# Head of a two-block transformer kernel: row copies on ScalarE, a norm product on GpSimd, ordered first loads, and unread TensorE products

## The chip, the cores and the metric

The kernel runs on one core of a Trainium2 chip. A core has five engines, each with its own queue of instructions: TensorE (PE, matrix products; its weight loads are listed apart as PEld), VectorE (DVE), ScalarE (ACT), GpSimd (POOL) and SyncE (SP), which here only issues DMA transfers. An engine works through its own queue in order, and instructions on different engines wait for each other through semaphores. TensorE reads its operands from SBUF and writes to PSUM, which has eight banks.

The metric is the device time in microseconds (us) of one run; the median over several runs is compared. One execution is recorded by the hardware profiler, and every duration quoted comes from it. The profile also shows the TensorE clock that was granted at each moment, as a share of full speed: 1.0 is full, 0.5 is half.

## The reference

The input is `x` of shape 32 x 64 x 512 (32 sequences of 64 tokens), one position for each token, and a conditioning vector of 512 numbers for each sequence. Everything is fp32. Two blocks follow each other:

```
# block 0
n(x, w, tw) = x * rsqrt(mean(x*x) + 1e-6) * (w * (1 + cond @ tw.T))
h = n(x, ln1_w, ln1_tw)
q, k, v = h @ Wq.T (8 heads of 64), h @ Wk.T, h @ Wv.T (one head)
q, k = rope(q, positions), rope(k, positions)
x = x + softmax(q k' / 8) v @ Wo.T
h = n(x, ln2_w, ln2_tw)
x = x + (silu(h @ Wg.T) * (h @ Wu.T)) @ Wd.T        # 512 -> 2048 -> 512
# block 1
scale, shift = split(cond @ W_ada.T + b_ada)
h = layernorm(x) * (1 + scale) + shift
q, c = h @ Wq.T (16 heads of 32), h @ Wkd.T (128)
k, v = c @ Wku.T, c @ Wvu.T (4 heads each)
x = x + softmax(rope(q) rope(k)' / sqrt(32)) v @ Wo.T
```

The four vectors that depend on `cond` (the scale of each of the two norms of block 0, and scale and shift of block 1) are called modulations 0 to 3 in the kernel.

## The kernel before, in words

**Tiling.** The 2048 tokens are cut into eight units of 256 tokens (four sequences). Channels lie on the 128 partitions, so a unit of `x` is a tile of 128 x 4 chunks x 256 tokens. Products are made in pieces: 128 x 128 weights against 256 tokens in the attention, against 128 in the MLP. The gate, up and down products of the MLP are computed by a scheme of seven products on blocks in place of eight. It needs sums and differences of weight blocks; `combine` (L255 to L258) makes them when a "set" of weights is used for the first time, in the first unit, and keeps them in DRAM. The sets pass through a ring of five buffers, tag `mw`. The first four weight tiles of the modulations (0 and 1) and the first sets share that ring.

**Stages.** The *head* is what runs before the first MLP product: modulations 0 to 3, the rotation angles, and block 0's attention for units 0 and 1. Then `Order().run` works through the MLP of unit after unit, with the attention of the neighbouring units woven in by estimated costs. The *tail* is block 1's attention for the last two units.

**What orders the head.** Three generators hand out TensorE work in pieces: `a` (attention of unit 0), `b` (attention of unit 1) and `m` (modulations 1 to 3). The string `FIRST` (L49) says in which order the next piece of each is taken, and the block `with ordered(tc, PE)` (L1045 to L1047) pins TensorE to that order. Modulation 0 stands before it. On the other four engines a scheduler orders the instructions, those of SP, which issues the transfers, among them.

**The parts that the text below speaks of**, with their lines in the kernel before:

- L152 to L154: eleven products of the constant tile `ones` with itself at the start; nobody reads the result.
- L175 (positions), L180 (`small`: conditioning vectors, mask and other small constants, 138 KB), L276 (weights of a modulation, two halves of 512 KB), L215 (`x` of a unit, 512 KB), L284 (`wqkv`: the weights of queries, keys and values, two tiles), L287 (`wo0`, 1 MB): the first loads. L242, L245 and L247 load the sets of MLP weights (L245 the block called `a21`).
- L290 to L315, `modulation`: sixteen products into `ps_mod` (L296), a copy of the result to SBUF as `rows` (L304), a transpose on TensorE (L307) and one VectorE instruction that leaves the modulation in its fixed tile (L311, L313 or L315).
- L364 to L395, `first_angles`: the angles of units 0 and 1, twenty small instructions on VectorE and ScalarE; L392 to L394 are `Abs` and the two sines, L395 the sine's sign.
- L498 to L520, `rms`: the square of `x` on ScalarE (L500) and the product of `x` and the modulation (L508). In the head ("lean") that product is made in two halves, one on VectorE and one on GpSimd, and the row factor, one over the root, is applied later (L521).
- L478, `root_by_quarters`: means over channels (`ms_a0` for unit 0) as small products; L470 the square root, L471 the reciprocal.
- L413 to L429, `tables_by_quarters`: L416 multiplies angles by the row factor, then TensorE spreads them (`tab`, `row`), and ScalarE copies them (L425, L426, L428).
- L525, `project`: the products of `kv`, `q` and `po` (the output projection). L533 to L536 rotate; L536, on GpSimd, leaves `qT`. L545 to L555 are the softmax. L673 are the scores. L560 are the transposes of the softmax result, `pp`. L573 adds `po` to `x`.
- L899 and L958: gate and up (`gu`) and down products of the MLP. L845, L869 and `lat` belong to block 1's attention.

**PSUM banks.** `abank(name)` hands out a bank from a list of homes in turn. In the head and in the tail the list is ("at", "gu", "acc", "acc"), in between it is "at" alone. How many tiles the head has taken therefore decides which home a later tile gets.

Of the kernel before, what the change touches and what calls it, by code (L numbers as in the profile page):

```python
# [17 lines left out]
P = 128  # L18
B, S, D = 32, 64, 512
T = B * S  # L20
KC = D // P
# [24 lines left out]
ROUND = 12582912.0  # L46
WARM = 11
STAY = 14103
FIRST = "aaaaaaa bb a mm aa bb a bbb aa b mm a bb aa a m b a b m b a b".replace(" ", "")  # L49
TWO_PI = float(np.nextafter(np.float32(2 * np.pi), np.float32(0)))  # L50


# [43 lines left out]
@contextmanager  # L96
def ordered(tc, engine):

    traced = tc.nc.cur_bb.bb.instructions
    start = len(traced)  # L100
    yield
    mine = [i for i in traced[start:] if i.engine == engine]
    info = mybir.DependencyInfo(mybir.DependencyClass.NoSync, mybir.DependencyReason.DATA)
    for one, other in zip(mine, mine[1:]):
        tc.add_manual_dep(other, one.name, info, reason="order")
# [3 lines left out]
def two_blocks(ctx: ExitStack, tc: tile.TileContext, a: dict, out: bass.AP):  # L109
    nc = tc.nc  # L110
# [8 lines left out]
    def bank(tag, name):  # L119
        return psum.tile([P, 512], F32, tag=tag, name=name, bufs=BANKS[tag])  # L120
# [12 lines left out]
    def fixed(shape):  # L133
        n, i = int(np.prod(shape[1:])), stays["at"]
        stays["at"] += n
        assert stays["at"] <= STAY
        t = stays["all"][:, i : i + n]
        if len(shape) == 2:
            return t
        names = "abc"[: len(shape) - 1]  # L140
        return t.rearrange(f"p ({' '.join(names)}) -> p {' '.join(names)}", **dict(zip(names, shape[1:])))

    def work(tag, shape, name, bufs=2):
        return wk.tile(shape, F32, tag=tag, name=name, bufs=bufs)
# [3 lines left out]
    make_identity(nc, ident)  # L148
    ones = fixed([P, P])
    nc.gpsimd.memset(ones, 1.0 / D)  # L150

    idle = bank("at", "idle")  # L152
    for _ in range(WARM):
        nc.tensor.matmul(idle[:, :P], ones, ones, start=True, stop=True)  # L154

    spread = fixed([P, US, P])
    nc.gpsimd.memset(spread, 0.0)
    for q in range(US):
        rows = slice(q * HALF0, (q + 1) * HALF0)
# [13 lines left out]
    def load_positions(u0):  # L173
        t = work("pos", [P, 2 * S], f"pos_{u0}", 1).bitcast(I32)
        nc.sync.dma_start(t, a["pos"][:, u0 * S : (u0 + 2) * S])  # L175
        positions.append(t)

    load_positions(0)
    small = fixed([P, C_ALL])
    nc.sync.dma_start(small, a["small"])  # L180
# [87 lines left out]
    def load_mod(i):  # L268

        mods.append({})  # L270
        for j, tag in enumerate((("mw", "mw"), ("mw", "mw"), ("h2", "h2"), ("sq", "td"))[i]):
            bufs = {"sq": 1, "mw": MW}.get(tag, 2)
            some = KC // 2 if tag == "td" else KC
            for k0 in range(0, KC, some):
                t = work(tag, [P, some, D // 2], f"mod_{i}_{j}_{k0}", bufs)
                nc.sync.dma_start(t, a["mod"][i][:, k0 : k0 + some, j * 256 : (j + 1) * 256])  # L276
                for k in range(some):
                    for c in range(2):
                        mods[i][2 * j + c, k0 + k] = t[:, k, c * P : (c + 1) * P]
# [5 lines left out]
    load_x(1)  # L285
    load_mod(1)
    nc.sync.dma_start(wo0, a["wo0"])  # L287


    def modulation(i):  # L290

        dst = (s0a, s0b, s1, t1)[i]
        ps = abank(f"ps_mod{i}")
        for k in range(KC):
            for c in range(KC):
                nc.tensor.matmul(  # L296
                    ps[c * B : (c + 1) * B, :P],
                    condT[:, k, :],
                    mods[i][c, k],
                    start=(k == 0),  # L300
                    stop=(k == KC - 1),
                )
        rows = work("latT1", [P, UT], f"rows_{i}", 1)[:, :P]
        nc.vector.tensor_copy(rows, ps[:, :P])  # L304
        yield 1.2, 0.5
        pt = abank(f"pt_mod{i}")
        nc.tensor.transpose(pt[:, :P], rows, ident)  # L307
        got = pt[:, :P].rearrange("p (c b) -> p c b", b=B)
        v = vecs[:, KC * i : KC * (i + 1)].unsqueeze(2).to_broadcast([P, KC, B])
        if i < 2:  # L310
            nc.vector.scalar_tensor_tensor(dst, got, 1.0, v, ALU.add, ALU.mult)  # L311
        elif i == 2:
            nc.vector.scalar_tensor_tensor(dst, got, 1.0, v, ALU.add, ALU.add)  # L313
        else:
            nc.vector.tensor_tensor(dst, got, v, ALU.add)  # L315
        yield 0.1, 0.0
# [115 lines left out]
    def per_seq(s, u):  # L432

        return s[:, :, US * u : US * (u + 1)].unsqueeze(3).to_broadcast([P, KC, US, S])

    def by_seq(ap):
        return ap.rearrange("p c (b s) -> p c b s", s=S)
# [14 lines left out]
    def tile4(room, tag, name):  # L452
        return space(room, tag, KC * UT, name).rearrange("p (c t) -> p c t", t=UT)

    def total_of(room, t, name):

        total = space(room, "tot", UT, f"tot_{name}")
        nc.gpsimd.tensor_tensor(t[:, 0:2], t[:, 0:2], t[:, 2:4], ALU.add)
        nc.gpsimd.tensor_tensor(total, t[:, 0], t[:, 1], ALU.add)
        return total  # L460

    def mean_of(parts, name):

        ps = abank(name)
        for k, part in enumerate(parts):
            nc.tensor.matmul(ps[:, :UT], ones, part, start=(k == 0), stop=(k == len(parts) - 1))
        return ps[:, :UT]

    def inverse_root(mean, eps, r):
        nc.scalar.activation(r, mean, AF.Sqrt, bias=eps)  # L470
        nc.vector.reciprocal(r, r)  # L471

    def root_by_quarters(parts, eps, r, name):

        ps = abank(name)
        for k, part in enumerate(parts):
            for b in range(US):
                nc.tensor.matmul(  # L478
                    ps[b * HALF0 : (b + 1) * HALF0, :S],
                    ones[:, :HALF0],  # L480
                    part[:, b * S : (b + 1) * S],
                    start=(k == 0),
                    stop=(k == len(parts) - 1),
                )
        inverse_root(ps[:, :S], eps, r)
# [9 lines left out]
    def rms(u, s, h, room, name):  # L495

        x = x_units[u]
        lean = "lean" in room  # L498
        sq = tile4(room, "h", f"sq_{name}") if lean else work("sq", [P, KC, UT], f"sq_{name}", 1)
        nc.scalar.activation(sq, x, AF.Square)  # L500
        if lean:
            parts = [sq[:, k] for k in range(KC)]
            c = KC // 2
            for e, part in ((nc.vector, slice(0, c)), (nc.gpsimd, slice(c, KC))):
                to = h[:, part].rearrange("p c (b s) -> p c b s", s=S)
                of = x[:, part].rearrange("p c (b s) -> p c b s", s=S)
                by = s[:, part, US * u : US * (u + 1)].unsqueeze(3).to_broadcast([P, c, US, S])
                e.tensor_tensor(to, of, by, ALU.mult)  # L508
            yield 0.0, 1.5
        else:  # L510
            parts = [total_of(room, sq, name)]
            nc.gpsimd.tensor_tensor(by_seq(h), by_seq(x), per_seq(s, u), ALU.mult)
            yield 0.0, 6.0
        if lean:
            return parts
        r = space(room, "r", UT, f"r_{name}")
        inverse_root(mean_of(parts, f"ms_{name}"), eps0, r)
        return r
# [61 lines left out]
    def attention0(u, room, early=None, late=None):  # L580
# [17 lines left out]
        def keys_values():  # L598
            kv = abank(f"kv0_{u}")
            project(kv[:, :UT], wqkv[0], slice(2 * P, 3 * P), h)  # L600
            return kv
# [7 lines left out]
        if lean:  # L609
            few = space(room, "few", 3 * S, f"quarters_{u}").rearrange("p (k c) -> p k c", c=S)  # L610
            root_by_quarters(r, eps0, few[:, 0], f"ms_a{u}")
            kv = keys_values()
            yield 1.7, 0.0
            turn = query(0)
            yield 3.4, 0.0
# [43 lines left out]
        if lean:  # L659
            ps = [space(room, "p", 512, f"p0_{u}_{t}") for t in range(2)]  # L660
        else:
            both = space(room, "p", 1024, f"p0_{u}")
            ps = [both[:, t * 512 : (t + 1) * 512] for t in range(2)]

        for ts in ((0,), (1,)) if lean else ((0, 1),):
            banks = [abank(f"sc0_{u}_{ts[0]}_{r}")[:, : 256 * len(ts)] for r in range(2)]
            for n in range(KC * len(ts)):
                t, c = ts[n // KC], n % KC
                for b in range(2):
                    cols = slice((2 * t + b) * S, (2 * t + b + 1) * S)  # L670
                    for r, sc in enumerate(banks):
# [5 lines left out]
                            start=True,  # L677
                            stop=True,
# [352 lines left out]
    for _ in modulation(0):  # L1031
        pass
# [7 lines left out]
    streams = {  # L1040
        "a": attention0(0, {"ring": "0", "lean": True, "p": [first[:, :512], first[:, 512:]]}, early),
        "b": ahead.pieces,
        "m": other_mods(),
    }
    with ordered(tc, mybir.EngineType.PE):  # L1045
        for name in FIRST:
            next(streams[name], None)  # L1047
    rest = [ahead]
    for w, key in ((wq1, "wq1"), (wkd, "wkd"), (wkv1, "wkv1"), (wo1, "wo1")):
        nc.sync.dma_start(w, a[key])  # L1050
# [144 lines left out]
```

## Time and profile before

| what | value |
|---|---|
| median of 3 runs | 1057.65 us (1056.87 to 1057.70) |
| the profiled execution | 1055.26 us |
| its span, first to last instruction | 1053.4 us |
| mean granted TensorE clock | 0.989 |
| TensorE busy | 1012.6 us, 96% of the span |
| VectorE, GpSimd, ScalarE busy | 546.7, 432.8, 329.1 us (52%, 41%, 31%) |
| the chain that ended last, by engine | TensorE 81%, VectorE 8%, GpSimd 5%, DMA 2% |
| first MLP product | 69.18 us after the span's start |

The span counts from the first to the last instruction of the execution; the 1.9 us around it belong to the run's time but to no instruction. The execution recorded was 2.4 us faster than the median of the three runs, so differences are worked out within the recorded execution and then applied to the median.

A line of the timeline gives start and duration in us, engine, source line, operation, the tile written and the tiles read with their shapes, and how many instructions were joined; brackets tell how long the engine stood idle before it and what released it. A line of the list of waits names the waiting instruction, what ended its wait, the total in us, the number, and the longest one. A line of the table of stretches gives start and end, length, TensorE's busy time there with the number of instructions, the granted clock, the busy share of the DMA engines (which can pass 1 a little, as packets overlap at its edges) and the GB/s moved.

### The profile page before, as it was taken

To read this page: it belongs to the slowest core of one execution; us is meant where nothing else is said; L and a number is where in the kernel's file an instruction comes from. 1 tells how busy PE (TensorE), PEld (TensorE's weight loads), DVE (VectorE), ACT (ScalarE), POOL (GpSimd) and SP (SyncE) were. 2 spreads that over 40 slices of the span, in tenths; PEclk is the share of its full clock that TensorE was granted. 3 is DMA by queue.
4 is the path that set the end of the run, shared out by engine and by line. 5 is a ranking of instruction groups with operands and counts; after the bars stand their busy time and mean duration, and the time that the engine had idled before them with its cause. 6 is when DMAs were issued, how large, how long until landed. Compare 5 with 4: busy or idle time off the path is not lost.

```text
span 1053.4 us, 21591 instructions
## 1 busy us (share of the span) xinstructions
PE 1012.6 (96%) x8602; PEld 938.7 (89%) x8602; DVE 546.7 (52%) x1377; ACT 329.1 (31%) x680; POOL 432.8 (41%) x518
## 2 busy tenths in 40 slices
PE   7899999999999999999999999999999999999887
PEld 6679999998999889989999989999999899999765
DVE  4966646545355385353555286532655345352363
ACT  4342112255114243142431332341424422141132
POOL 3424545443255443355341544234632335432541
PEclk8989999999999999999999999999999999999899
DMA  8816896463666364663555565465735547564001
GB/s 277 310 61 218 288 303 247 151 211 122 234 210 211 108 244 152 219 243 127 212 178 181 207 209 183 141 214 187 277 117 194 202 165 280 204 229 170 11 1 40
DMA packets 68275, 198.55 MB, mean 188 GB/s; under 512 B 7248, under 2 KB 15184, under 8 KB 67792
## 3 DMA queue, kind: packets, MB, share of 16 engines
q1 hardware_dynamic: 68176, 197.17, 53.4%
q8 instruction: 69, 1.13, 0.4%
q14 instruction: 30, 0.25, 0.1%
HBM read 180.37 MB, written 16.78 MB: 187 GB/s over the span
## 4 chain that ended last, share of the span: by engine, by line
PE 81%; DVE 8%; POOL 5%; DMA 2%; issue 2%; ACT 1%; SPq 0%; ACTq 0%; POOLq 0%; DVEq 0%
PE gu L899 34%; PE down L958 17%; PE po L525 10%; PE q L525 9%; DMA set<-in_wmlp 2%; PE cx L869 2%; PE sc L845 1%; PE lat L525 1%; PE pp L560 1%; PE sc L673 1%; PE kv L525 1%; PE cx L694 1%; DVE sm L553 1%; PE tab L400 1%; DVE mx L545 1%
## 5 line engine op out<-in xcount | busy, mean ns | idle before, releaser
L899 PE MATMUL gu<-h,set 128*128 128x128 f32 x2048 | 288.1, 277 | 6.4 <-DVE c L918 5.7
L899 PEld LDWEIGHTS gu<-h,set 128*128 128x128 f32 x2048 | 258.8, 192 | 15.5 <-issue 10.4
L899 PE MATMUL gu<-hc,set 128*128 128x128 f32 x1536 | 215.2, 275 | 0.0
L899 PEld LDWEIGHTS gu<-hc,set 128*128 128x128 f32 x1536 | 193.5, 192 | 1.0 <-issue 0.6
L937 POOL TENSOR_TENSOR act<-c,c 128x384 f32<-128x384 f32 x64 | 66.4, 1038 | 210.5 <-DVE c L925 140.8
L958 PE MATMUL down<-td,set 128*128 128x128 f32 x1024 | 137.5, 276 | 3.3 <-POOL td L940 2.5
L958 PEld LDWEIGHTS down<-td,set 128*128 128x128 f32 x1024 | 125.4, 192 | 5.2 <-POOL td L940 3.5
L911 ACT COPY e<-gu 128x128 f32<-128x128 f32 x128 | 33.7, 264 | 259.9 <-PE gu L899 246.8
L525 PE MATMUL q<-h,stays 128*128 128x256 f32 x480 | 111.3, 385 | 1.5 <-POOL h L774 1.5
L525 PE MATMUL po<-cT,stays 128*128 128x256 f32 x480 | 109.0, 382 | 2.1 <-DVE sm L553 2.1
L958 PE MATMUL down<-act,set 128*128 128x128 f32 x768 | 109.5, 278 | 0.0
L925 DVE TENSOR_TENSOR c<-gu,u 128x256 f32<-128x256 f32 x128 | 53.4, 419 | 106.4 <-PE gu L899 106.1
L525 PEld LDWEIGHTS q<-h,stays 128*128 128x128 f32 x480 | 90.9, 193 | 14.3 <-POOL h L774 1.7
L525 PEld LDWEIGHTS po<-cT,stays 128*128 128x128 f32 x480 | 89.8, 191 | 14.0 <-ACT cT L878 2.6
L958 PEld LDWEIGHTS down<-act,set 128*128 128x128 f32 x768 | 97.6, 192 | 5.2 <-issue 3.2
L913 DVE TENSOR_TENSOR u<-e,gu 128x128 f32<-128x128 f32 x128 | 35.9, 281 | 127.5 <-ACT e L911 126.8
L555 POOL TENSOR_TENSOR p<-p,sm 128x512 f32<-128x512 f32 x40 | 41.6, 1058 | 121.4 <-DVE sm L554 113.7
L536 POOL TENSOR_TENSOR qT<-u_q,v_q 128x512 f32<-128x512 f32 x30 | 38.1, 1269 | 97.2 <-DVE v_q L535 97.1
L573 DVE TENSOR_TENSOR x<-x,po 128x512 f32<-128x512 f32 x32 | 22.0, 687 | 87.7 <-PE po L525 87.7
L994 ACT ACT_TABLE_LOAD x34 | 43.6, 1283 | 54.5 <-DVE c L925 54.0
L939 POOL TENSOR_TENSOR td<-act 128x256 f32<-128x256 f32 x64 | 46.7, 730 | 5.6 <-DVE act L936 0.9
L994 ACT ACTIVATE c<-gu 128x128 f32<-128x128 f32 x64 | 17.7, 277 | 90.2 <-DVE c L925 82.2
(269 smaller groups left out, 1333.0 us busy)
## 6 DMA issues: line engine op xcount, KB each, us to landing
set<-sums SPq DMA_DIRECT2D x168, 512.0 KB, 5.6
set<-in_wmlp SPq DMA_DIRECT2D x192, 384.0 KB, 4.6
sums<-set SPq DMA_DIRECT2D x24, 512.0 KB, 4.1
x<-in_x SPq DMA_DIRECT2D x8, 512.0 KB, 5.5
out_x<-x SPq DMA_DIRECT2D x16, 256.0 KB, 2.3
mod<-in_mod SPq DMA_DIRECT2D x7, 512.0 KB, 5.2
a<-in_wmlp SPq DMA_DIRECT2D x24, 128.0 KB, 3.1
stays<-in_wo SPq DMA_DIRECT2D x2, 1024.0 KB, 8.0
```

The lines of the kernel that those rows point to most:

```text
L525: nc.tensor.matmul(ps, w[:, k, cols], h[:, k, :], start=(k == 0), stop=(k == KC - 1))
L536: nc.gpsimd.tensor_tensor(dst, u, v, ALU.add)
L555: nc.gpsimd.tensor_tensor(p8, p8, sm.unsqueeze(2).to_broadcast(wide), ALU.mult)
L573: nc.vector.tensor_tensor(x[:, part], x[:, part], po, ALU.add)
L899: nc.tensor.matmul(ps, w[:, slot, k * P : (k + 1) * P], b[of][:, k], start=start and k == 0, stop=k == 1, skip_group_check=True)
L911: nc.scalar.copy(e, ps[:, 0])
L913: nc.vector.tensor_tensor(u2, e, ps[:, 1], ALU.add)
L925: nc.vector.tensor_tensor(c.rearrange("p (a b) t -> p a b t", b=2)[:, :, 1], ps[:, 2:4], u2.unsqueeze(1).to_broadcast([P, 2, HT]), ALU.add,)
L937: nc.gpsimd.tensor_tensor(act[:, 1:4], gate[:, 1:4], c[:, 1:4], ALU.mult)
L939: nc.gpsimd.tensor_tensor(td[:, 0:2], act[:, 1:3], act[:, 0:2], ALU.subtract)
L958: nc.tensor.matmul(sums_of[u][p][:, c], w[:, slot, c * P : (c + 1) * P], b[of], start=q % NP == 0 and i % 2 == 0 and c == 0, stop=q % NP = ...
L994: nc.scalar.activation(gate[2][:, 0], gate[0][:, 0], AF.Silu)
```

## The change

There are five edits, all in the head:

1. The copies of the four modulations' `rows` are made by ScalarE (`nc.scalar.copy`) instead of VectorE.
2. For unit 0 of block 0's first norm (name `a0`) both halves of `h` are multiplied by GpSimd; unit 1's halves stay divided.
3. The loads from the first positions to `wo0` are issued in the order in which they are written: positions, `small`, first and second half of modulation 0, `x` of unit 0, `wqkv` 0, `wqkv` 1, `x` of unit 1, modulation 1, `wo0`. Before, the order that SP had was positions, first half of modulation 0, `small`, second half, `x` of unit 0, `wqkv` 0, `x` of unit 1, `wqkv` 1.
4. The unread products become a function `idle(n)`, which takes a bank by `abank` each time. It is called with 11 at the start as before, with 2 in modulation 0 after the copy of its rows (TensorE meets these two after the first two products of that modulation), with 4 for unit 0 between the means and the keys and values, and with 2 at three more places of `FIRST`, marked `i`: before the transpose of modulation 3, and two before the spreading of unit 1's second row factor.
5. As each call takes a bank, the later tiles of the head, and those of the tail, lie two places further in the rotation of homes.

Nothing that reaches the output is computed differently. The diff, cut to its core:

```
-FIRST = "aaaaaaa bb a mm aa bb a bbb aa b m a bb aa a m b a b m b a b".replace(" ", "")
+FIRST = "aaaaaaa bb a mm aa bb a bbb aa b m a bb aa a m b a bi m b ii a b".replace(" ", "")
...
-    idle = bank("at", "idle")
-    for _ in range(WARM):
-        nc.tensor.matmul(idle[:, :P], ones, ones, start=True, stop=True)
+    idles = {"n": 0}
+
+    def idle(n):
+
+        idles["n"] += 1
+        ps = abank(f"idle_{idles['n']}")
+        for _ in range(n):
+            nc.tensor.matmul(ps[:, :P], ones, ones, start=True, stop=True)
+
+    idle(WARM)
...
+    first_loads = ExitStack()
+    first_loads.enter_context(ordered(tc, mybir.EngineType.SP))
     load_positions(0)
...
     nc.sync.dma_start(wo0, a["wo0"])
+    first_loads.close()
...
-        nc.vector.tensor_copy(rows, ps[:, :P])
+        nc.scalar.copy(rows, ps[:, :P])
+        if i == 0:
+            idle(2)
...
-            for e, part in ((nc.vector, slice(0, c)), (nc.gpsimd, slice(c, KC))):
+
+            for e, part in ((nc.gpsimd if name == "a0" else nc.vector, slice(0, c)), (nc.gpsimd, slice(c, KC))):
...
             root_by_quarters(r, eps0, few[:, 0], f"ms_a{u}")
+            if u == 0:
+                idle(4)
             kv = keys_values()
...
         for name in FIRST:
-            next(streams[name], None)
+            if name == "i":
+                idle(2)
+            else:
+                next(streams[name], None)
```

More of the change, by code (lines that the diff above doesn't have):

```diff
@@ L48 @@
 STAY = 14103
-FIRST = "aaaaaaa bb a mm aa bb a bbb aa b mm a bb aa a m b a b m b a b".replace(" ", "")
+FIRST = "aaaaaaa bb a mm aa bb a bbb aa b mm a bb aa a m b a bi m b ii a b".replace(" ", "")
 TWO_PI = float(np.nextafter(np.float32(2 * np.pi), np.float32(0)))
```

## Prediction

> **What bounds the kernel now.** I read the page's parts 1 and 4 first: TensorE is busy for 96% of the span and holds 81% of the chain, so time saved anywhere else counts only where TensorE waits or runs slowly. Everything the diff names lies in the head, before the first gate and up products at 69.18 us, so next I read the timeline there, the chain of waits, and the table of stretches for the granted clock.
>
> TensorE's first large wait, in the list of waits from 0 to 48 us:
>
> ```profile
> PEld kv L525 <- DVE h L508: 2.6, 1, 2.6
> PE kv L525 <- DVE h L508: 2.3, 1, 2.3
> ```
>
> Keys and values wait for the half of `h` that VectorE multiplies. The timeline (start, duration) shows why that half is late:
>
> ```profile
> 10.42 0.28 DVE L304 COPY rows<-ps_mod 128x128 f32<-128x128 f32 x1
> 11.33 0.29 DVE L311 SCALAR_TENSOR_TENSOR stays<-pt_mod,stays 128x128 f32<-128x128 f32 x1 [0.36 <-PE pt_mod L307]
> 11.71 2.05 POOL L508 TENSOR_TENSOR h<-x,stays 128x512 f32<-128x512 f32 x2 [6.42 <-DVE stays L311]
> 12.72 1.12 DVE L395 TENSOR_TENSOR stays<-few 128x64 f32<-128x64 f32 x1 [0.99 <-ACT few L394]
> 13.90 0.68 DVE L508 TENSOR_TENSOR h<-x,stays 128x512 f32<-128x512 f32 x1
> 14.63 3.06 PEld L525 LDWEIGHTS kv<-h,stays 128*128 128x128 f32 x8 [2.56 <-DVE h L508]
> 14.64 3.78 PE L525 MATMUL kv<-h,stays 128*128 128x256 f32 x8 [2.33 <-DVE h L508]
> 18.21 4.72 PE L525 MATMUL q<-h,stays 128*128 128x256 f32 x16
> 24.50 3.67 PE L525 MATMUL q<-h,stays 128*128 128x256 f32 x16
> 28.68 1.99 PE L525 MATMUL kv<-h,stays 128*128 128x256 f32 x8
> ```
>
> The product for modulation 0 ended at 8.52, but its copy stood behind the angle work on VectorE until 10.42; then L395 (angles) lay before L508. And the same 8 and 16 pieces that take 1.99 and 3.67 us later took 3.78 and 4.72 here. The table of stretches tells why (start:end, length, TensorE busy, granted clock, DMA share, GB/s):
>
> ```profile
> 6.83:10.24 3.41, 1.07 (x28) 0.99 0.96 390
> 10.24:13.65 3.41, 1.46 (x33) 0.50 1.02 395
> 13.65:17.07 3.42, 2.43 (x6) 0.50 1.09 365
> 17.07:20.48 3.41, 3.41 (x10) 0.51 0.68 251
> 64.85:68.27 3.42, 1.38 (x13) 0.99 0.00 0
> 68.27:71.68 3.41, 3.26 (x20) 0.51 0.02 5
> 986.44:989.86 3.42, 1.95 (x40) 0.99 0.02 5
> 1013.75:1017.16 3.41, 1.82 (x9) 1.00 0.00 0
> ```
>
> The clock changes only at steps of about 3.41 us. It fell after steps with 1.07, 1.38 and even 1.95 us of (small) products, held after one with 1.82 us of large ones, and returned after a full one, not after one with 2.43.
>
> **Part 1, rows copied by ScalarE, and `small` loaded second.** ps_mod0 still ends at 8.52: it waits for the second half of mod 0, which landed at 7.4 with the same bytes ahead. `small` (138 KB) goes ahead of 512 KB; it landed at 5.5, and by the rate of 330 GB/s between 3 and 6 us should land near 3.5, so the angles start 2 us sooner and VectorE is free for L311. A ScalarE copy of this size takes 0.27 (rows of L911): 8.57 to 8.84; the transpose 0.33; L311 near 9.3 to 9.6 instead of 11.33 to 11.62.
>
> **Part 2, both halves of the first `h` on GpSimd.** x0 lands at 9.4 as before. Two products of 1.03 each (2.05 for two, above) run from about 9.65 to 11.7; the first chunk pair is there at 10.7, but wqkv0, issued at 3.78 and 7.5 us to landing, is not before 11.3. The small constants (eps, the quarter turn) now follow these products on GpSimd; behind them wait ScalarE's cosines (L393), the square root's table load (1.28) and L470 (0.31), then L471 and L416 on VectorE. GpSimd's half for unit 1 waits for x1, now behind wqkv1 (13.9 instead of 12.55); nothing needs it before 23.
> [...]
>
> **Part 3, unread products in the head.** One takes 2 pieces of 0.137 us warm (rate of L899), 0.226 cold (22 pieces in 4.97 us at the start). idle(2) of modulation 0 falls into the wait for mod 0's second half (to 7.45) and costs nothing. idle(4) stands after ms_a0 (sq_a0 ends at 10.5; 0.65 us warm, to 11.15) and before kv: 8 x 0.137 = 1.1, to 12.25. From h and wqkv0 kv could start at 11.3, so it costs 0.95. Still kv moves from 14.64 to 12.25.
> What it buys rests on the clock. The step to 10.24 now holds about 0.45 (idle) + 1.07 + 0.25 (transpose) = 1.77 us of busy TensorE, between the 1.38 that lost the clock and the 1.82 that kept it. [...]
>
> **Part 4, what follows.** From 24.64 to 48 VectorE is the chain, almost without a pause. Two copies (0.28 each) leave it: +0.3 to the scores. But not all transfers move. combine(0) on GpSimd waits for a21_0 until 19.2 in both; then qT (1.27) and two steps of combine(1) put the end of L257 at 24.95, only 4.5 earlier than 29.48. SP issues a21_3 after that, and the change puts mod 2's second half (512 KB, 1.3 us at 400 GB/s) between a21_3 and wo0, set 3. Before, set 3 landed 6.5 us after a21_3's issue (30.37 + 5.6 = 36.0), and L255 needed it at 37.02. Now it lands at 24.95 + 7.8 = 32.75, and is wanted at 37.02 - 5.3 = 31.7: **-1.1**, with VectorE's softmax sums queued behind it, and GpSimd and the transposes behind those (bounds 0 and -2).
> The rows of modulation 2 leave VectorE, where they held the transpose to 50.39 behind a mask step of 1.29 (L333): **+0.6**. ScalarE's copy of the rows of modulation 3 comes between sq_b and the square root, on the chain 61.7 to 66.0: **-0.26**.
> The last three idle(2): 12 pieces, 1.65 warm. The first delays the transpose and pp by 0.55, to 65.46; the others end at 66.55, before row_b (66.71) may start; without that wait they would cost the 1.1. They leave the step before gu with some 2.7 us of work, so gu starts warm. Its first 8 pieces took 2.08; warm 1.1, but then they wait for L734 (70.40). po follows at 72.05 instead of about 72.8: **+0.75**.
> Bank rotation: the extra tiles move the later ones by two places. In the tail the second q of unit 7 must now wait for the first softmax subtraction of unit 6 (1012.95 instead of 1011.95): 1.0 later, hidden, as TensorE then idles 2.3 us before pp. lat and q of unit 6 swap order, with equal work: 0.
>
> **Sum:** 5.0 + 0.3 - 1.1 + 0.6 - 0.26 + 0.75 = 5.3 us. The profiled execution took 1055.26 (span 1053.4 and 1.9 around it) and would take 1050.0; the median shown, 2.4 higher, becomes 1057.65 - 5.3 = **1052.3**. After 69 us each TensorE instruction only moves earlier, and the weight loads follow its releases.
>
> **Rivals.** [...] (c) The change does nothing for the time: transfers set the head (DMA share about 1.0 from 3 to 19 and 31 to 56), and set 3's wait takes all; 1057.2. Against it: only one of them is on the chain, by 1 us. (d) Slower: moved by 1.5 steps against the clock, the tail (1013 to 1043, steps with 1.7 to 2.5 us of work that just hold it) loses it. A lost step costs at most 1.7; from four of them on (6.8) the gain of 5.3 is gone, five make 1060.9. Against it: two neighbours would each have to fall below what has held so far.
>
> **How the numbers follow.** Forecast case 0.50 (own range 1051.0 to 1053.8), (a) 0.28, (b) 0.12, (c) 0.06, (d) 0.04. The range: below, the forecast with set 3 in time (+1.1) and part of what the clock may return at po (up to 1.0, 51 to 55 us) and at 990 (up to 1.4): 1049.6; above, (b) with set 3 at its bound: 1056.3. About 0.2%, 2.1 us, is what a measurement can tell here: faster by more, below 1055.5: 0.50 + 0.28 + 0.08 = 0.86; within, 0.09; slower, 0.05.
>
> **What would show it.** Right: kv at 12.2 to 12.5 with a granted clock of 1.0, tables near 17.8, L255 of set 3 waiting for DMA near 32, gu at 64 to 65 at full clock. Wrong: a clock of 0.5 between 10 and 17; kv waiting for GpSimd's second product; tables waiting for L416; or an equal head with steps of half clock after 1010.

## The result

The changed kernel takes **1054.62 us** (1052.73 to 1056.52), the kernel before 1057.64 us (1056.87 to 1059.37): ratio 0.9971, 95% interval 0.9956 to 0.9986, or 3.0 us less. Measured once more beside other runs of before, the ratio was 0.9967 (0.9953 to 0.9981). The forecast was 1052.3, the range 1049.6 to 1056.3: the sign and the range held, but of the 5.3 us only 3 to 3.5 came.

The experiments below find that two of the five edits, the rows on ScalarE and the first `h` on GpSimd, bring 6.6 us by themselves, and that the other three together take back about half of that. That the sum landed in the range is therefore in part luck.

The recorded execution of the changed kernel took 1055.98 us, that of before 1055.26. So this pair shows the change as 0.7 us *slower*, while the medians show it 3 us faster. Where that comes from is part of what the experiments had to find.

The timeline of the changed kernel, in the places shown of before (start, duration, engine, line):

```profile
8.25 1.07 PE L305 MATMUL ps_mod<-mod,stays 128*32 128x128 f32 x28 [0.30 <-DMA mod<-in_mod]
9.36 0.27 ACT L313 COPY rows<-ps_mod 128x128 f32<-128x128 f32 x1 [3.42 <-PE ps_mod L305]
10.12 0.29 DVE L322 SCALAR_TENSOR_TENSOR stays<-pt_mod,stays 128x128 f32<-128x128 f32 x1 [1.67 <-PE pt_mod L318]
10.55 2.06 POOL L520 TENSOR_TENSOR h<-x,stays 128x512 f32<-128x512 f32 x2 [5.45 <-DVE turns L401]
11.22 1.16 PE L158 MATMUL idle<-stays 128*128 128x128 f32 x8
11.68 1.00 DVE L401 TENSOR_TENSOR turns<-few,turns 128x64 f32<-128x64 f32 x1
12.22 1.89 PE L537 MATMUL kv<-h,stays 128*128 128x256 f32 x8
13.95 3.62 PE L537 MATMUL q<-h,stays 128*128 128x256 f32 x16
15.85 0.29 DVE L427 TENSOR_TENSOR quarters<-stays,quarters 128x128 f32<-128x128 f32 x1
17.40 1.05 PE L411 MATMUL tab<-quarters,stays 128*128 128x128 f32 x8
...
33.90 0.43 DVE L263 TENSOR_TENSOR set<-a,set 128x256 f32<-128x256 f32 x1 [2.35 <-DMA set<-in_wmlp]
34.24 1.27 DVE L565 TENSOR_REDUCE sm<-p 128x8 f32<-128x512 f32 x2
37.00 0.66 PE L572 MATMUL pp<-stays,p 128*128 128x128 f32 x4 [2.76 <-POOL p L567]
```

`kv` starts at 12.22 instead of 14.64 and takes 1.89 us instead of 3.78, `q` 3.62 instead of 4.72: full clock. The tables start at 17.40 instead of 22.77. Then VectorE waits 2.35 us for set 3, the softmax sums (L565) are queued behind it, and the first transpose `pp` comes at 37.00 instead of 40.45. The lead of 5.4 us has become 3.4. The same places in the kernel before, where set 3 had landed when VectorE (L255) came to it:

```profile
22.77 1.05 PE L400 MATMUL tab<-quarters,stays 128*128 128x128 f32 x8
37.02 0.42 DVE L255 TENSOR_TENSOR set<-a,set 128x256 f32<-128x256 f32 x1
40.45 0.66 PE L560 MATMUL pp<-stays,p 128*128 128x128 f32 x4 [0.33 <-POOL p L555]
69.18 2.08 PE L899 MATMUL gu<-h,set 128*128 128x128 f32 x8
```

The first `gu`, in the last of these lines at half clock, is at full clock in the changed kernel:

```profile
66.84 1.16 PE L913 MATMUL gu<-h,set 128*128 128x128 f32 x8 [0.48 <-DVE h L533]
```

How the lead goes on, by the starts of the same TensorE instructions in the two records:

| instruction | before | after | lead |
|---|---|---|---|
| `kv` | 14.64 | 12.22 | 2.42 |
| `tab` | 22.77 | 17.40 | 5.37 |
| first `pp` | 40.45 | 37.00 | 3.45 |
| transpose of modulation 2 | 50.39 | 46.68 | 3.71 |
| `po` of unit 0 | 52.97 | 49.86 | 3.11 |
| products of modulation 3 | 60.84 | 58.41 | 2.43 |
| first `gu` | 69.18 | 66.84 | 2.34 |
| `po` of unit 1 | 72.67 | 69.56 | 3.11 |
| `gu` in the first MLP unit | 106.65 | 103.20 | 3.45 |
| `gu` behind its last new set | 155.29 | 154.28 | 1.01 |
| `gu` | 398.11 | 398.38 | -0.28 |
| second `q`, unit 7 | 1011.95 | 1012.22 | -0.27 |
| `pp`, unit 6 | 1017.87 | 1017.00 | 0.87 |
| last `po` | 1049.23 | 1050.04 | -0.81 |

Beyond the head nothing was edited but the banks of some tiles in the tail, yet 4 us go there: 2.4 between 107 and 150 us, 1.2 near 395, 0.4 near 585 and 1.7 at 1030, with a gain of 1.5 near 990 between them. The table of stretches (start:end, length, busy time of TensorE, of its weight loads, of VectorE, ScalarE and GpSimd, then granted clock, DMA share and GB/s) shows what happens near 395, first in the changed kernel, then before:

```profile
387.32:390.73 3.41, 2.98 (x27) 2.79 (x25) 3.38 (x11) 1.24 (x4) 0.71 (x1) 1.00 0.01 2
390.73:394.15 3.42, 1.24 (x9) 1.03 (x10) 3.42 (x14) 0.00 (x0) 1.37 (x2) 1.00 0.73 265
394.15:397.56 3.41, 3.41 (x18) 3.41 (x18) 2.05 (x9) 1.49 (x3) 0.00 (x0) 0.50 0.26 93
```

```profile
388.80:392.20 3.40, 2.60 (x24) 2.41 (x23) 3.37 (x11) 0.95 (x3) 1.04 (x1) 1.00 0.01 2
392.20:395.70 3.50, 1.70 (x14) 1.50 (x15) 3.47 (x16) 0.00 (x0) 1.04 (x1) 1.00 0.71 262
395.70:399.10 3.40, 3.23 (x29) 2.99 (x28) 2.46 (x9) 2.61 (x6) 0.17 (x1) 1.00 0.61 225
```

Both kernels have the same pause here, in a softmax of the second unit's work. In the changed kernel's record it lies in one step of the clock, which holds 1.24 us of work, and the next step is granted at half speed: 1.2 us lost. In the record of before it is divided between two steps with 2.60 and 1.70, and nothing is lost.

### The profile page after: what moved, and what is told of

It is laid out like the page before. It is cut to its first block, busy times and chain, and to the rows that moved or that the text cites. A ratio compares the mean times of both kernels' runs of the same rounds, so it can differ in the third digit from the quotient of the medians.

```text
span 1054.2 us, 21632 instructions
## 1 busy us (share of the span) xinstructions
PE 1014.2 (96%) x8626; PEld 940.2 (89%) x8626; DVE 546.1 (52%) x1372; ACT 329.9 (31%) x684; POOL 434.2 (41%) x519
## 4 chain that ended last, share of the span: by engine, by line
PE 80%; DVE 6%; POOL 5%; DMA 5%; issue 2%; ACT 1%; SPq 0%; ACTq 0%; POOLq 0%; DVEq 0%
PE gu L913 33%; PE down L972 16%; PE po L537 10%; PE q L537 9%; DMA set<-in_wmlp 3%; PE cx L883 2%; PE pp L572 1%; PE sc L859 1%; PE lat L537 1%; PE sc L687 1%; DMA a<-in_wmlp 1%; PE cx L708 1%; PE kv L537 1%; DVE sm L565 1%; DMA mod<-in_mod 1%
## 5 line engine op out<-in xcount | busy, mean ns | idle before, releaser
L537 PE MATMUL po<-cT,stays 128*128 128x256 f32 x480 | 111.3, 388 | 2.1 <-ACT cT L892 2.1
L537 PE MATMUL q<-h,stays 128*128 128x256 f32 x480 | 109.0, 380 | 0.0
```

What stands on the lines that cost most here:

```text
L537: nc.tensor.matmul(ps, w[:, k, cols], h[:, k, :], start=(k == 0), stop=(k == KC - 1))
```

## The experiments

The runs form three groups, each with its own runs of the kernel before; ratios are to those runs, with their 95% interval. Where two ratios are compared, their uncertainty is the root of the sum of the squares of the two half-widths. The times in the profile lines come from one execution of each kernel.

### Did the loss after the head belong to the change?

Theory T1: the transfers of the first MLP unit take back what the head gives. Rival T2: what was lost there belonged to that execution, and the head's lead carries through.

**The changed kernel once more.**

> The changed kernel once more, for a second record of it. Theory T1 (the transfers of the first MLP unit take back what the head gives): the lead over the recorded execution of the kernel before is 3 to 3.5 us at 105 us and about 1 us at 155 us, as in the first record (3.45 and 1.01). Rival T2 (the loss between 107 and 150 us belonged to that one execution; the lead of the head carries through): the lead at 155 us is 2.5 to 3.5. Time by both 0.9956 to 0.9986 of before.

Measured: 1053.04 us against 1056.38, ratio 0.9967 (0.9953 to 0.9981). Its record is very different from the first:

```profile
5.96 0.41 PE L305 MATMUL ps_mod<-mod,stays 128*32 128x128 f32 x4
9.20 1.92 PE L305 MATMUL ps_mod<-mod,stays 128*32 128x128 f32 x28 [2.18 <-DMA mod<-in_mod]
15.32 2.03 PE L537 MATMUL kv<-h,stays 128*128 128x256 f32 x8
36.92 0.42 DVE L263 TENSOR_TENSOR set<-a,set 128x256 f32<-128x256 f32 x1 [2.81 <-DMA set<-in_wmlp]
40.02 1.12 PE L572 MATMUL pp<-stays,p 128*128 128x128 f32 x4 [2.88 <-POOL p L567]
```

The second half of modulation 0 came at 9.20, not 8.25, and the clock had fallen: the 28 products took 1.92 us instead of 1.07. `kv` started at 15.32, later than before the change. The table of stretches has the reason, a step with 1.55 us of work, the two unread products of modulation 0 among it (four pieces):

```profile
5.36:8.77 3.41, 1.55 (x12) 1.00 (x11) 3.00 (x10) 0.51 (x4) 0.00 (x0) 1.00 1.04 363
8.77:12.18 3.41, 2.37 (x29) 1.54 (x29) 0.12 (x1) 1.02 (x2) 0.00 (x0) 0.50 1.01 401
```

The lead over the record of before was only 1.77 at 105 us and 0.73 at 155; 1.2 us went at 394.5 as in the first record. But no step was lost at 990, which gained 3.1 us on the record of before, nor at 1030, and the end came 2.4 us before that record's. So neither theory's numbers came: two records of the same kernel differ by 3 us at `kv`, at the tables and at the first `pp`.

**A delay of 2.8 us ahead of the first MLP products.**

```
-        for name in FIRST:
+        for at, name in enumerate(FIRST):
             if name == "i":
-                idle(2)
+                idle(14 if at == FIRST.rindex("i") else 2)
```

> The changed kernel with 14 instead of 2 unread products at the last place before the spreading of the second row factor: the first gate and up products start 2.8 us later (69.6 instead of 66.84), all else equal. T1: the transfers between 110 and 150 us decide, the delay is gone by 155 us, and the time is 0 to 0.8 us above the changed kernel. T2: the delay carries through, the time is 2.3 to 2.8 us above, that of the kernel before or 0.5 below it.

Measured: 1055.26 us, 0.9985 (0.9972 to 0.9998), 2.2 us above the changed kernel of the same group. Between `cx` and the spreading of the second row factor lie 5.25 us instead of 3.26, so the delay was 2.0 and not 2.8: part of the added products filled a wait that was there before. About as much was paid, but the two ratios differ by 0.0018 with an uncertainty of 0.0019, so the time alone decides little.

The records decide more. DMA stands still from 60 to 75 us (share 0.00 to 0.02 in the first records of both kernels), and the first transfer after that is issued at 75.89 in the changed kernel, behind the first `gu`. So a later head moves these transfers too. And what is lost from 107 to 150 us does not follow the lead: against the first record of before it is 2.4 and 1.0 us in the two records of the changed kernel, 2.2 in this one, but 0.3 in the kernel without unread products (below), which came with the second largest lead, 6.6, and kept 6.1 of it to the last `po`. T1 falls. T2 holds only in part, as some us are lost at places that change from record to record.

**The kernel before once more.**

> The kernel before once more, for a second record. If the low clock of its head belongs to the kernel: a fall at 8 to 11 us and half clock for two or three steps, kv at 14 to 15, tables at 21.5 to 23. If it depended on where the clock's steps lay: full clock at 10 to 17 and tables at about 20. In the tail, with steps lying elsewhere, another set of lost steps than 989.8 to 996.6.

Measured: 1056.54 against 1056.21, ratio 1.0009 (0.9994 to 1.0024), which is how well such a comparison repeats. Its record took 1059.33 us, 4.1 more than the first. `kv` came at 14.93, the tables at 21.92, with half clock for three steps from 8.2 us, where the first record has three from 10.2: the slow head belongs to the kernel, not to one execution. But the second half of modulation 0 came at 8.78 and not at 7.45, and further steps were lost at 254, 397, 1022 and 1032.

### What did the unread products bring, and what the order of the sums?

**No unread products after the start.**

```
-        for _ in range(n):
+        for _ in range(n if n == WARM else 0):
```

> The changed kernel without the unread products after the start (the eleven at the start stay, and so does the rotation of banks). If they hold the clock: kv starts at about 11.3 but at half clock or loses it by 17, tables at 18.5 to 21 instead of 17.4, the first gu pieces are slow again, and the time is 1 to 3 us above the changed kernel. If they do nothing but cost 0.95 us in front of kv: tables at 16.4, and the time is equal or up to 0.9 below the changed kernel.

Measured: 1051.98 us, 0.9952 (0.9934 to 0.9971). The clock held in the head without them: `kv` started at 11.26, the tables at 16.68, and the first `pp` at 33.82. But the run was not the clean one it was meant to be. With the products gone, the scheduler had put set 3's sums behind the softmax sums on VectorE:

```profile
11.26 2.14 PE L537 MATMUL kv<-h,stays 128*128 128x256 f32 x8 [0.35 <-POOL h L520]
31.02 1.46 DVE L565 TENSOR_REDUCE sm<-p 128x8 f32<-128x512 f32 x2
33.76 1.29 DVE L263 TENSOR_TENSOR set<-a,set 128x256 f32<-128x256 f32 x1 [1.04 <-DMA set<-in_wmlp]
33.82 0.66 PE L572 MATMUL pp<-stays,p 128*128 128x128 f32 x4
```

**All unread products, with the order of that run.** An ordering dependency holds the first two sums of set 3 behind the second reciprocal of unit 0's softmax; VectorE, ScalarE, GpSimd and SP then have the order of the run without unread products, so the two differ only in these products.

```
...
+            if n == 3:
...
+                for one in sums:
+                    tc.add_manual_dep(one, made["0_0_1", 0], info, reason="order")
...
```

> The changed kernel, all unread products kept, with VectorE's first two sums of set 3 behind the two softmax sums and reciprocals of unit 0 instead of ahead of them; VectorE, ScalarE, GpSimd and SP then have exactly the order of the run without unread products. Theory S (what that run gained over the changed kernel came from this order, not from the missing products): the first softmax transpose at 34 to 35 instead of 37.0 to 40.0, a lead of the head larger by 2 to 2.5 us than in the changed kernel, time about 1051, within 0.8 us of the run without unread products. Rival U (the missing products brought it): time 1052.5 to 1053.5, as the changed kernel.

Measured: 1052.53 us, 0.9954 (0.9937 to 0.9971). From the tables to the first `pp` it is 16.3 us (19.20 to 35.53), where the changed kernel has 19.6 and 19.4; the wait for set 3 is 0.68 us and holds no softmax:

```profile
19.20 1.05 PE L419 MATMUL tab<-quarters,stays 128*128 128x128 f32 x8
34.97 0.66 DVE L265 TENSOR_TENSOR set<-a,set 128x256 f32<-128x256 f32 x1 [0.68 <-DMA set<-in_wmlp]
35.53 0.61 PE L583 MATMUL pp<-stays,p 128*128 128x128 f32 x4
```

The pair 0.9952 and 0.9954 shows no worth of the unread products in the time; the intervals leave room for some 2.6 us either way. In this record the clock fell at 12.0 in spite of them. The three late ones do what they were counted for: `gu` had full clock in six of the seven records with them (its first eight pieces in 1.16 us; 1.71 in "`wo0` later"), and half clock in all seven without (2.07 or 2.08 us). Between 8 and 18 us half clock came in three of the seven records with unread products (changed again and sums behind by the granted clock; loads free by its products alone, 28 of which took 1.92 us there) and in six of the seven without (all but "no unread"). So they may well hold the clock more often, but so few records, of kernels that differ in other edits too, cannot settle it. The four before `kv` cost some 0.6 us: GpSimd's first product ends near 11.6 in the changed kernel, and `kv` starts at 12.22. The order of the sums shows clearly in the records, by 3 us from the tables to the first transpose, but not in the time: 0.9954 against 0.9967, with intervals that overlap widely.

**`wo0` behind sets 3 and 4.**

> The changed kernel with wo0 (1 MB) loaded behind sets 3 and 4 instead of ahead of them. Set 3 lands at about 31 instead of 33.9, VectorE's 2.35 us wait for it goes to 0 to 0.5, the first transpose of the softmax moves from 37.0 to about 35.2, gu from 66.84 to about 65.0. T1: most of these 1.8 us are lost again before 155 us, time 0 to 0.6 below the changed kernel. T2: 1.8 below it.

Measured: 1052.47 us, 0.9960 (0.9948 to 0.9972). Set 3 landed at 33.49, the wait was 1.81 us, `pp` came at 36.92. Moving 1 MB away brought 0.8 us from issue to landing (6.4 after 7.3), not 3: the expectation was wrong. One reason lies in the order of SP: with `wo0` gone, it issued 64 KB of positions (25.92) and 512 KB of modulation weights (26.58) ahead of set 3 (27.05), which in the changed kernel stood behind it. More than half of the 1 MB was replaced.

**Both, without unread products.**

> No unread products after the start, sums of set 3 behind the softmax sums, and wo0 loaded behind sets 3 and 4. If set 3 is what still holds VectorE (1.04 us at 33.76 in the run without unread products): that wait goes to 0 to 0.4 and the time is 0.4 to 1 us below that run. If its landing is set by the rate of the transfers and not by wo0 (33.9 became only 33.5 when wo0 was moved): no difference, 0 to 0.3 us.

Measured: 1055.43 us, 0.9986 (0.9974 to 0.9999), 3.5 us more than without the edit, against both expectations. The line shows why: the scheduler now put the first sum of set 4 ahead of the softmax sums, and it waited for its small block:

```profile
37.59 0.43 DVE L265 TENSOR_TENSOR set<-a,set 128x256 f32<-128x256 f32 x1 [5.05 <-DMA a<-in_wmlp]
40.70 1.11 PE L582 MATMUL pp<-stays,p 128*128 128x128 f32 x4 [5.13 <-POOL p L577]
```

This is the clearest run on the point: one sum stands in front of two softmax sums and waits 5.05 us for 128 KB, and the first transpose comes 6.9 us later than at 33.82. Of these, 2.4 were lost ahead of the tables (19.06 instead of 16.68), where the clock had fallen.

### Which edit brought the 3 us?

**The first transfers not in the given order.**

> The changed kernel without the given order of the first transfers: first half of modulation 0 ahead of the small constants, x of unit 1 ahead of the second wqkv tile, as before the change. If the given order delays modulation 0 (its second half landed at 7.45 before and at 7.9 to 9.2 in the records of the changed kernel): it lands at 7.3 to 7.6 again, its products end at 8.5, and kv starts 0.3 to 1 us sooner than 12.2, while the angles end 2 us later; time 0 to 1 us below the changed kernel if the tables (17.4) don't wait for the angles, up to 1 above if they do. If the landing varies by itself: 7.5 to 9.2, and kv at 12 to 13.

Measured: 1053.61 us, 0.9966 (0.9953 to 0.9979), no different from the changed kernel. This is not the order of before, as was expected: SP now issued the first half of modulation 0, positions, the second half, and only then `small`. The products waited for these constants until 7.99, `kv` started at 15.84 and the tables at 21.78, 4.4 us later than in the changed kernel. But GpSimd's order had changed as well: it made the sums of the second set before the first `qT`. So SP issued set 3 at 26.47, where the changed kernel has 26.62, and it was there in time:

```profile
7.99 0.64 PE L302 MATMUL ps_mod<-mod,stays 128*32 128x128 f32 x4 [1.80 <-DMA stays<-in_small]
26.47 5.01 SPq L248 DMA_DIRECT2D set<-in_wmlp  x2
35.18 0.41 DVE L261 TENSOR_TENSOR set<-a,set 128x256 f32<-128x256 f32 x1
38.59 0.66 PE L569 MATMUL pp<-stays,p 128*128 128x128 f32 x4 [0.32 <-POOL p L564]
```

`pp` came at 38.59, only 1.6 later. That the first `gu` then comes at 66.84, the very time of the changed kernel, is chance: that record loses two steps of the clock from 46 us on, this one a single one. The run says that the given order of loads is not needed for the gain. It does not say that an earlier head only waits longer for set 3: between the two records of the changed kernel the tables lie 3.2 us apart, and set 3's issue (26.62 and 29.01) and the first `pp` (3.0) move with them.

**The rows copied by VectorE again.**

```
-        nc.scalar.copy(rows, ps[:, :P])
+        nc.vector.tensor_copy(rows, ps[:, :P])
```

> The changed kernel with the four copies of the rows on VectorE again, all else kept. The copy of modulation 0 stands behind angle work again, but that starts with the earlier small constants: modulation ready at 10.5 to 11.5, kv at 12.5 to 14, one to two us later than 12.2, and the four copies (0.28 each) return to VectorE: time 1 to 2.5 us above the changed kernel (0.998 to 0.9995 of before). If the copies were not what held the head: no difference, 0.9967.

Measured: 1056.0 us, 0.9994 (0.9978 to 1.001): nearly all of the gain is gone, though the first `h` is still made by GpSimd alone. The start of the head is little worse (`kv` 12.86, tables 18.29), but the transposes of modulations 1 and 2 wait 1.69 and 3.16 us for their rows instead of 0.39 and 1.98, and in this record a step of the clock is lost at 30.8 besides (a `q` of 5.41 us instead of 3.72).

**The rows on ScalarE alone**, everything else as before the change:

> The kernel before with the rows copied by ScalarE and nothing else (the scheduler then puts set 3's sums behind the softmax sums, as in the run of that name). If the copy behind the angle work on VectorE was what held the head: the modulation is ready at 9.4 to 10.5 instead of 11.6, VectorE's half of h follows at once, kv starts at 11.3 to 12.5 with or without full clock, the head leads by 2 to 4 us, time 2 to 3.5 us below before (0.9968 to 0.998). If GpSimd's takeover or the given order of transfers is needed for it: 0 to 1 us.

Measured: 1052.44 us against 1057.29, 0.9955 (0.9943 to 0.9968), 4.8 us: no less than the whole change brings. `kv` at 12.00, tables at 19.74:

```profile
9.56 0.27 ACT L304 COPY rows<-ps_mod 128x128 f32<-128x128 f32 x1 [1.25 <-PE ps_mod L296]
11.26 0.69 DVE L508 TENSOR_TENSOR h<-x,stays 128x512 f32<-128x512 f32 x1
```

The order of the sums is part of it, since the scheduler answers to this edit by putting set 3's sums behind the softmax; how large a part, no run tells.

**Both halves of the first `h` on GpSimd alone:**

> The kernel before with both halves of unit 0's h multiplied by GpSimd and nothing else. The modulation stays at 11.3 to 11.6, GpSimd's two products end at 13.7 and kv starts then instead of at 14.64: 0.9 us in the head, time 0 to 1 us below before (0.999 to 1.0). If VectorE's half in the angle work was the cause by itself: kv at 12.5 or earlier and 2 us or more.

Measured: 1053.56 us, 0.9969 (0.9957 to 0.998), 3.3 us by the ratio, with set 3's sums still in front: the expectation of 0 to 1 us was far too low. The lines tell what was overlooked:

```profile
11.89 3.06 POOL L508 TENSOR_TENSOR h<-x,stays 128x512 f32<-128x512 f32 x3 [6.59 <-DVE stays L311]
12.99 3.69 PE L525 MATMUL kv<-h,stays 128*128 128x256 f32 x8 [0.51 <-POOL h L508]
```

`kv` takes the chunks of `h` in order, and needs the first two first. Those were VectorE's, late; now GpSimd makes them first (11.89 to 12.9), and the other two are made while `kv` works on the first. So `kv` starts 1.65 us earlier, not 0.9, and the clock comes back at 16.4 instead of 20.4: the tables are 2.8 us earlier.

**Both of these edits, and nothing else:**

```
-        nc.vector.tensor_copy(rows, ps[:, :P])
+        nc.scalar.copy(rows, ps[:, :P])
...
-            for e, part in ((nc.vector, slice(0, c)), (nc.gpsimd, slice(c, KC))):
+            for e, part in ((nc.gpsimd if name == "a0" else nc.vector, slice(0, c)), (nc.gpsimd, slice(c, KC))):
```

> The kernel before with the rows copied by ScalarE and both halves of unit 0's h on GpSimd; no given order of transfers, no unread products, the old rotation of banks. If these two are the whole of the change's effect: 1052 to 1053.5, 0.995 to 0.997 of before. If the order of transfers carries a part: 1054 or more.

Measured: **1050.72 us, 0.9937 (0.9915 to 0.9958)**, 6.6 us below before and faster than the changed kernel (0.0030 below its 0.9967, with an uncertainty of 0.0026). Behind the eleven at the start it has no unread product:

```profile
10.87 2.06 POOL L508 TENSOR_TENSOR h<-x,stays 128x512 f32<-128x512 f32 x2 [5.78 <-DVE turns L390]
11.97 3.04 PE L525 MATMUL kv<-h,stays 128*128 128x256 f32 x8
18.30 1.05 PE L400 MATMUL tab<-quarters,stays 128*128 128x128 f32 x8
34.65 0.66 PE L560 MATMUL pp<-stays,p 128*128 128x128 f32 x4
```

All records of the head together (start in us; the second column is the start of modulation 0's second group of products, which waits for its second half, or in "loads free" for the constants; "front" and "behind" say where set 3's sums stand relative to unit 0's softmax sums):

| kernel | mod 0 | `kv` | `tab` | `pp` | `gu` | sums | ratio |
|---|---|---|---|---|---|---|---|
| before | 7.45 | 14.64 | 22.77 | 40.45 | 69.18 | front | 1 |
| before, again | 8.78 | 14.93 | 21.92 | 39.59 | 68.47 | front | 1.0009 |
| changed | 8.25 | 12.22 | 17.40 | 37.00 | 66.84 | front | 0.9971 |
| changed, again | 9.20 | 15.32 | 20.64 | 40.02 | 68.53 | front | 0.9967 |
| delay | 7.96 | 12.15 | 17.33 | 37.28 | 67.73 | front | 0.9985 |
| `wo0` later | 8.86 | 12.83 | 18.01 | 36.92 | 64.34 | front | 0.9960 |
| both, no unread | 8.17 | 12.04 | 19.06 | 40.70 | 69.39 | set 4's in front | 0.9986 |
| loads free | 9.72 | 15.84 | 21.78 | 38.59 | 66.84 | front | 0.9966 |
| rows on VectorE | 8.10 | 12.86 | 18.29 | 38.13 | 68.63 | front | 0.9994 |
| a0 alone | 8.07 | 12.99 | 19.97 | 37.88 | 65.77 | front | 0.9969 |
| sums behind | 7.67 | 12.60 | 19.20 | 35.53 | 64.32 | behind | 0.9954 |
| no unread | 7.86 | 11.26 | 16.68 | 33.82 | 62.95 | behind | 0.9952 |
| rows alone | 8.45 | 12.00 | 19.74 | 36.15 | 63.18 | behind | 0.9955 |
| rows and a0 | 8.48 | 11.97 | 18.30 | 34.65 | 62.64 | behind | 0.9937 |

From the tables to the first `pp` it is 18.9 to 20.0 us in the first four kernels that have all the edits and set 3's sums in front (changed, again, delay, `wo0` later), and 16.3 to 17.1 in all four with the sums behind. In both records of before, "a0 alone" and "loads free", where the sums stand in front too, it is 16.8 to 17.9: there set 3 had landed when VectorE came to it. In "rows on VectorE" (19.8) it had not.

## Why the prediction was right, and where it was wrong

The forecast saw rightly what held the head, VectorE's queue in front of the first `h`. Its sum rested on the clock that the unread products were to hold, and it took the order of VectorE's sums as it found it. The runs give the two first edits more than it forecast for all of them, and the rest a cost that it did not have; that the two errors partly cancel, and leave a time inside the range, is luck.

**Part 1 (rows on ScalarE)** named the right cause: a small copy behind angle work on VectorE held the head. Alone it is worth 4.8 us, the reordered sums included. Its times were too early, L311's successor at 10.12 and not 9.3 to 9.6, because the step "ps_mod0 still ends at 8.52", "with the same bytes ahead", failed: it ended at 9.32. The landing at 7.45 in the record of before was a single draw: in the thirteen records in which TensorE waited for it, it lay between 7.45 and 9.20, and at 8.78 in the second one of before.

**Part 2 (GpSimd)** was right in the start of `kv`: 12.25 forecast, 12.22 recorded. The angles did run longer beside GpSimd's products (10.55 to 12.61): L401, which reads two tiles, took 1.00 us from 11.68 and 0.22 from 10.32, and its neighbour L400, which reads one, 0.94 from 10.71 and 0.19 from 8.26. In the record of before it was L395, with 1.12 us from 12.72, beside such a product, and 0.21 from 14.50. The quarters were nevertheless ready at 16.14, before TensorE ended `q` at 17.57, so this cost nothing. What the part didn't count is the value of having the *first* half early by itself, 3.3 us in the run of that edit alone.

**Part 3 (unread products)** was right in the record (tables at 17.40, forecast near 17.8) and wrong as a reason. The 5.0 us that the sum gives the head up to the tables, and the rival (b) at the upper end of the range, were the author's estimates, and no run shows them as such: the lead at the tables was 5.37 us in the first record of the changed kernel and 2.13 in the second. The step that failed took the position of the clock's steps from the one record of before, with an edge at 10.24, and asked whether 1.77 us of work would hold *that* step. Edges lay elsewhere in each execution: 8.44 and 11.86 in the first record of the changed kernel, where the clock stayed at 1.00 after steps with 1.91 and 2.40 us of work, 8.77 in the second, where it fell to 0.50 after one with 1.55 (TensorE's longest gap about it was 2.2 us, from 7.01 to 9.20). As the steps of 3.41 us lay differently in each record, the prediction should have weighed the clock over all positions of the edge instead of over one. Rivals (a) and (b), with a fall of the clock in the head, were thus not other theories but other draws of the same kernel. In the time the unread products brought nothing that could be measured.

**Part 4.** Set 3's wait was mis-sized. The lead first grew from 5.37 at the tables to 5.9 at the scores (forecast +0.3) and then fell to 3.45 at `pp`: 2.4 us, where 1.1 was forecast, as set 3 landed at 33.90 and not 32.75 and VectorE wanted it at 31.55. The rows of modulation 2 gave 0.60 as forecast (lead 3.11 to 3.71), and full clock at `gu` gave 0.77 (2.34 to 3.11; forecast 0.75). Not counted were two lost steps from 46.0 on, where before had lost one at 51.15: 1.3 us (3.71 to 2.43). So 5.3 had become 3.1 at 70 us. Tail: the second `q` of unit 7 lost 1.1 us to the new bank rotation and `pp` had it back, as forecast.

**"After 69 us each TensorE instruction only moves earlier"** failed. Moved work meets the clock's steps at another place, and what is lost from 107 to 150 us varies; that changes the end by some us either way in one execution. The medians over many executions show 3.0 to 3.5 us, where the recorded pair shows nothing.

**Where the rest went.** Rows and GpSimd together bring 6.6 us, the whole change 3.0 to 3.5. So the other edits (unread products, order of loads, rotation) take back about 3. A second pair of one group says the same: "rows on VectorE" has GpSimd's edit and these three and stands at 0.9994, "a0 alone" has only GpSimd's and stands at 0.9969; the difference, 0.0025, has an uncertainty of 0.0020. And "loads free" (0.9966) has the rows, GpSimd's edit, unread products and rotation, so the given order of loads is not needed for the loss.

One carrier is shown in the records: with the unread products the scheduler has set 3's sums in front of the softmax sums, where they wait 2.35 and 2.81 us in the two records of the changed kernel. In the time it is not shown: undoing only that order made 0.9967 into 0.9954, within the intervals. The rest, some 1.8 us between "sums behind" and "rows and a0", whose intervals overlap too, stays open. So does the loss between 107 and 150 us: it was -0.3 to 2.4 us in the twelve records with an edit, 1.3 on average, and 0.2 in the second record of before.

Rival (c), that the transfers take it all, is true of a part: in the changed kernel set 3 took 2.4 of the lead of 5.9. The given order of the first loads brought nothing that could be measured ("loads free", 0.9966). Rival (d) named a real mechanism, the tail losing clock steps (one at 1029.0 in the first record, 1.7 us), but as a lasting shift; it is a draw, and it strikes before as well (1021.9 and 1032.2 in its second record).

## What to carry to other kernels

Look for the small copy that stands in an in-order queue behind work it has nothing to do with, and give the consumer's first chunk to the engine that is free first: two such one-line edits were worth about twice the full change. When an edit changes the instructions that a scheduler weighs, look at the order of *all* engines afterwards, above all for an instruction that waits for a transfer in front of one that is ready. And don't tune against a clock edge seen in one record: here the same pause near 390 us cost a step of half clock in the first record of the changed kernel (394.15 to 397.56) and none in the first of before.

## What was not expected of the hardware

- In the first records of before and of the changed kernel, what the clock did after a step went with TensorE's busy time in it. The two hold 600 whole steps of 3.41 us at full clock. All 6 with less than 1.5 us of busy TensorE (0.84 to 1.47) were followed by half clock, none of the 575 with more than 2.4 us was, and of the 19 between these 2 were (1.95 us in the step from 986.4 of before, 1.89 in the step from 988.1 of the changed kernel), while the least that held had 1.61. In the changed kernel's step from 390.73 the longest pause was 1.8 us, and the clock fell.
- The same transfer of 512 KB, issued in the first 3 us with the same bytes ahead within each kernel, let its products start between 7.45 and 8.78 in the two records of before, and between 8.25 and 9.20 in the two of the changed kernel. The delayed kernel, whose head is the same up to there and which ran on the same chip as the record with 9.20, had 7.96.
- Single executions of one kernel lay between 1049.33 and 1056.06 us (the changed one, measured again), twice the effect of the whole change.
